# Attention's k, V and q in a pool of their own, loaded ahead; waits by tile; last additions on VectorE

## The chip, the cores and the metric

The kernel runs on one core of a Trainium2 chip. The metric is the device time of one execution in microseconds, from the median of several runs. The engines have their own instruction queues: TensorE (PE, with its weight loads as PEld), VectorE (DVE), ScalarE (ACT), GpSimd (POOL), and SyncE (SP), which here only issues transfers (DMA).

## The reference, cut to what matters

The input x is 4 x 128 x 64 x 64, in float32. Two layers follow each other.

Layer 0 normalises x by groups, runs small state-space models (a seed and a cascade of two) over the 4096 positions, and ends with a convolutional FFN per batch entry: a 128 to 256 matmul, a 3 x 3 depthwise convolution, GELU and a 256 to 128 matmul.

Layer 1 is attention and a mixture of experts over the 4096 tokens of each batch entry:

```python
t = _to_tokens(x)
t = t + _L1_attn_ref(_ln_t(t), ...)   # 4 heads of 32, softmax over 4096 keys
t = t + _L1_ffn_ref(_ln_t(t), ...)    # 8 experts of 128 to 128, top 2
```

with, inside attention,

```python
scores = jnp.einsum('bhqd,bhkd->bhqk', q, k) / jnp.sqrt(jnp.float32(HEAD_DIM))
attn = jax.nn.softmax(scores, axis=-1)
ctx = jnp.einsum('bhqk,bhkd->bhqd', attn, v)
```

## The kernel before

**Layer 0** (L1154). Positions are cut into 8 blocks of 512. The scan over seed and cascade goes block by block. The operations are recorded by a planner (`Deck`, L773): steps of several generators are interleaved by `run` (L255) in proportion to the number of steps that each is given, every recorded operation gets its place in that order as its rank, and `flush` (L911) lays the operations out with assumed costs and emits them. The emitted order is kept on PE, DVE, ACT and POOL (`manual_schedule`, L1490); SP is not in that list, so the order of its transfers is set by the framework. In the profile every recorded operation has line L1040.

The FFN of a batch entry (`ffn`, L1357) runs beside the scan of the next one. The last FFN, that of entry 3, has no scan beside it. There it is interleaved with attention's projections of entry 0 (`early`, L1526, which steps through `prepare`, L1574): for each block of 512 tokens a normalisation, then q, k and V, where q and k are split into a high part and a low part (`lower`, L1609), and all are stored in DRAM (qd, kd, vd). The FFN is entered in the interleaving with 129 steps, the projections with 47 (L1542). The pools for this part (`first`, `psf`, `last`, L1519 and L1520) are opened after those of the scan are closed (L1518). The FFN of a block ends with a sum t (L1472 on DVE, L1473 on POOL) and its store to td.

**Layer 1** (L1646). A unit is one head and one block of 512 queries: 4 entries x 8 blocks x 4 heads = 128 units. `load` (L1814) fetches a unit's keys k4 (four strips of 32 partitions, two with the high part and two with the low part, 512 KB each), its queries q4 (four strips) and its values V. For every unit there are three passes:

- maxima: 32 matmuls of 128 queries by 512 keys, each reduced on DVE (`maximum`, L1836), 44 of them ahead of the first group (LEAD);
- scores in 8 groups of 512 keys (`scores`, L1874): a matmul that subtracts the maximum (L1882), four score matmuls (L1888), the exponential on ACT (L1892), and the sums over the group's four parts on POOL (L1894, L1896), which later give the denominator;
- context: e times V (L1909), and the denominator from the sums (`total`, L1918). Both are saved to DRAM (`save`, L1901).

When the four heads of a block are done, `tail` (L1696) reads their parts back (L1699), adds the parts (L1705 to L1712), multiplies by the inverse of the denominator (L1714), applies the output projection, a second normalisation (with a product, L1733) and the experts (L1774 to L1788), and stores the block. The steps of tails and of the next entry's projections are fitted between the groups by `background` (L1946). After the loop over the groups, the first steps of the last tail are emitted and then the rest:

```python
for _, task in timed:
    next(task)
behind += [start(task) for _, task in soon]
while behind:
    advance(behind)
```

`timed` holds five steps of the last tail, which are five of its six sums, and `start` takes the sixth. `behind` holds what is left of the tail of the block before.

The constants of layer 1 (pc, 906.5 KB) are loaded twice: for the early projections on POOL's queue (L1522), and for layer 1 on ACT's (L1675).

Of the kernel before, what the change touches and what calls it, by code (L numbers as in the profile page):

```python
# [21 lines left out]
F32 = mybir.dt.float32  # L22
# [4 lines left out]
AX = mybir.AxisListType  # L27
ENG = mybir.EngineType
PSUM = bass.MemoryType.PSUM

NBATCH, C, IMG = 4, 128, 64
L = IMG * IMG
# [1117 lines left out]
def blk(k):  # L1150
    return slice(k * LB, (k + 1) * LB)


def layer0(tc, T, td, const, ident, eps, where, batches, qkv):  # L1154
# [9 lines left out]
    with ExitStack() as ctx:  # L1164
# [139 lines left out]
        class Cascade(Seed):  # L1304
# [194 lines left out]
        for s in range(-2, len(items) + 1):  # L1499
# [12 lines left out]
            if 0 < s and items[s - 1].last:  # L1512
                if pending is not None:
# [35 lines left out]
class Stores:  # L1549


    def __init__(self, pool):
        self.pool, self.q, self.k, self.v = pool, {}, {}, {}
# [92 lines left out]
def layer1(tc, T, td, const, ident, eps, where, out, batches, qkv):  # L1646
# [10 lines left out]


    nc = tc.nc
    NQT = L // 128  # L1660
    LEAD = 44
    with ExitStack() as ctx:
        fix = ctx.enter_context(tc.tile_pool(name="fix1", bufs=1))
        kvp = ctx.enter_context(tc.tile_pool(name="kv", bufs=3))
        work = ctx.enter_context(tc.tile_pool(name="work1", bufs=2))
        dram = ctx.enter_context(tc.tile_pool(name="dram1", bufs=2, space=bass.MemoryType.DRAM))
        psm = ctx.enter_context(tc.tile_pool(name="psm", bufs=3, space=PSUM))
        pss = ctx.enter_context(tc.tile_pool(name="pss1", bufs=2, space=PSUM))
        psa = ctx.enter_context(tc.tile_pool(name="psa", bufs=1, space=PSUM))
# [26 lines left out]
        def tail(b, k):  # L1696
            pa = work.tile([128, 2, 4, LB], F32, tag="parts", bufs=1, name="parts")
            for h in range(NHEAD):
                nc.sync.dma_start(out=pa[HD * h:HD * h + HD], in_=cds.pop((b, h, k)).rearrange("s i d l -> d s i l"))  # L1699
            tk = tmp("tt", bufs=2)  # L1700
            nc.sync.dma_start(out=tk, in_=td[b, :, blk(k)])
            cx = tmp("cx", bufs=1)
            for s in (1, 0):
                yield
                nc.gpsimd.tensor_add(pa[:, s, 0], pa[:, s, 0], pa[:, s, 1])  # L1705
# [4 lines left out]
                nc.gpsimd.tensor_add(pa[:, s, 2], pa[:, s, 2], pa[:, s, 3])  # L1710
                yield
                nc.gpsimd.tensor_add(pa[:, s, 0], pa[:, s, 0], pa[:, s, 2])  # L1712
            yield 0.4, False
            nc.gpsimd.tensor_mul(cx, cx, pa[:, 0, 0])  # L1714
            yield 0.0, False
            yield 0.75, True
            po = ps("ps_o")
# [12 lines left out]
            r = tmp("r")  # L1730
            rsqrt(nc, r, pv, eps)
            yield 0.4, False
            nc.gpsimd.tensor_mul(xl, xl, r)  # L1733
            yield 0.0, False
            yield 0.8, True
            pl = ps("ps_l")[:, 0:4 * NEXP]
# [77 lines left out]
        def load(u):  # L1814

            if u >= len(units):
                return
            b, h, k = units[u]
            if h == 0 and k == 0:
                while ahead or todo:  # L1820
                    if not ahead:
                        ahead.append(start(todo.pop(0)))
                    advance(ahead)
            k4 = kvp.tile([128, L], F32R, tag="k4", name="k4")
            for j in range(4):
                nc.sync.dma_start(out=k4[32 * j:32 * j + 32, :].bitcast(F32),
                                  in_=qkv.k[b][j // 2, HD * h:HD * h + HD, :])
            q4 = work.tile([128, LB], F32R, tag="q4", bufs=5, name="q4")
            for j in range(4):
                nc.sync.dma_start(out=q4[32 * j:32 * j + 32, :].bitcast(F32),  # L1830
                                  in_=qkv.q[b][j % 2, HD * h:HD * h + HD, blk(k)])
            V = kvp.tile([128, NQT, HD], F32, tag="V", name="V")
            nc.sync.dma_start(out=V.rearrange("p t d -> p (t d)"), in_=qkv.v[b][h])
            k4s[u], q4s[u], Vs[u] = k4, q4, V

        def maximum(n):  # L1836

# [36 lines left out]
        def scores(u, g, n):  # L1874

            pts = [pss.tile([128, 2, LB], F32, tag="s", name="ps_s") for _ in range(2)]
            for j in range(4):  # L1880
                rows = slice(32 * j, 32 * j + 32)
                nc.tensor.matmul(pts[j // 2][:, j % 2, :], lhsT=ones2[rows, :], rhs=mrows[u][rows, :],  # L1882
                                 start=True, stop=False)
            for j in range(4):
                if j % 2 == 0:
                    maximum(n + j // 2)
                kt = 4 * g + j
                nc.tensor.matmul(pts[j // 2][:, j % 2, :], lhsT=k4s[u][:, 128 * kt:128 * kt + 128],  # L1888
                                 rhs=q4s[u], start=False, stop=True)
# [6 lines left out]
            nc.gpsimd.tensor_add(s, s2[:, 0], s2[:, 1])  # L1896
            return e, s

        accs, dens = {}, {}
# [113 lines left out]
def emit(tc, T, where, out, batches=range(NBATCH), layers=(0, 1), td=None):  # L2013
    nc = tc.nc
    with ExitStack() as ctx:
        cp = ctx.enter_context(tc.tile_pool(name="const", bufs=1))
        ct = cp.tile([128, where["const"]["grp"][0]], F32, name="const_sb")
        nc.gpsimd.dma_start(out=ct, in_=T["const"][:, 0:where["const"]["grp"][0]])
        const = Cols(ct, where["const"])
        ident = cp.tile([128, 128], F32, name="ident")  # L2020
        make_identity(nc, ident)
        eps = cp.tile([128, 1], F32, name="eps")
        nc.gpsimd.memset(eps, 1e-5)
        qkv = Stores(ctx.enter_context(tc.tile_pool(name="qkv", bufs=2, space=bass.MemoryType.DRAM)))
# [21 lines left out]
```

## Time and profile before

| | |
|---|---|
| median of 3 runs | 8313.97 us (8304.8 to 8316.73) |
| the profiled execution | 8310.76 us, of which the span 8309.0 us |
| granted TensorE clock, mean | 0.954 |
| busy: PE, DVE, ACT, POOL | 91%, 76%, 61%, 59% of the span |
| layer 0, scan | up to about 3472 us |
| last FFN with the projections | about 3472 to 3672 us |
| attention: first maximum, first scores | 3694.0 us, 3722.4 us |
| last scores | 8248.7 us |
| POOL addition 128x1024, 128x512 (L1894, L1896) | 2385 ns, 1281 ns, 1024 of each |
| DVE maximum 128x512 (L1852) | 689 ns, 4096 of them |

The span is the profiler's, from the first to the last instruction. Times of single instructions are given in us from its start. A row of the chain or of the timeline gives start, duration, engine, tile and line, and where there is a mark "x8" the number of instructions that were merged. DMA issues appear on the queue that issues them (SPq, ACTq, POOLq) with the time of the issue, not of the transfer.

### The profile page before, as it was taken

The numbers are of one execution on the slowest core, as the hardware profiler recorded it, in microseconds if no ns is written. First come the engines' busy times: TensorE is split into PE (matmuls) and PEld (weight loads), VectorE is DVE, ScalarE is ACT, GpSimd is POOL, SyncE is SP. The second block draws the span as 40 slices with busy tenths as digits, with TensorE's granted clock in tenths as the row PEclk, the third lists the DMA queues.
The fourth block names the chain that finished last, engine by engine and source line by source line (L and its number), as shares of the span: only waits on it lengthen the run. The fifth ranks groups of instructions, "written<-read, shape, count | busy, mean of one in ns | idle before, by whom it ended". The sixth has DMA issues, their size and how long they took to land.

```text
span 8309.0 us, 191474 instructions
## 1 busy us (share of the span) xinstructions
PE 7600.4 (91%) x80284; PEld 4516.6 (54%) x80284; DVE 6299.9 (76%) x11211; ACT 5103.8 (61%) x6517; POOL 4892.5 (59%) x3441
## 2 busy tenths in 40 slices
PE   5888888888888898779999999999999999999998
PEld 3566666666666666434555555555555545555554
DVE  5676768887888788776777777777777777777775
ACT  5767767777777777545555555555555555555554
POOL 1111111211122112119999999999999999999997
PEclk7889999999999899889999999999999999999999
DMA  4221112221112121145544445444545454444442
GB/s 139 83 56 48 43 53 57 54 57 54 52 55 59 54 62 46 54 133 139 129 126 124 127 123 130 127 126 126 129 121 136 122 135 122 120 116 121 116 121 59
DMA packets 306606, 800.55 MB, mean 96 GB/s; under 512 B 43985, under 2 KB 61009, under 8 KB 288849
## 3 DMA queue, kind: packets, MB, share of 16 engines
q1 hardware_dynamic: 304848, 780.94, 35.8%
q8 instruction: 633, 10.37, 0.5%
q10 hardware_dynamic: 432, 5.12, 0.2%
q14 instruction: 229, 1.87, 0.1%
q0 software_dynamic: 464, 2.25, 0.1%
HBM read 595.19 MB, written 192.94 MB: 95 GB/s over the span
## 4 chain that ended last, share of the span: by engine, by line
PE 29%; POOL 22%; issue 3%; DVE 2%; ACT 1%; DMA 1%; SPq 0%; POOLq 0%; DVEq 0%
POOL s L1894 13%; PE ps_mx L1850 7%; PE acc L1909 6%; POOL es L1896 6%; PE ps_s L1888 6%; PE ps_s L1882 3%; PE ps_e L1798 2%; PE ps_den L1922 1%; DVE mx L1852 1%; PE ps_taps L1040 1%; PE ps_sh L1869 0%; POOL parts L1712 0%; POOL cx L1714 0%; PE ps_f L1787 0%; PE ps_f L1786 0%
## 5 line engine op out<-in xcount | busy, mean ns | idle before, releaser
L1852 DVE TENSOR_REDUCE mx<-ps_mx 128x1 f32<-128x512 f32 x4096 | 2789.8, 689 | 815.0 <-PE ps_mx L1850 807.8
L1892 ACT ACTIVATE e<-ps_s 128x1024 f32<-128x1024 f32 x2048 | 1985.3, 1022 | 1715.6 <-PE ps_s L1888 1610.8
L1894 POOL TENSOR_TENSOR s<-e 128x1024 f32<-128x1024 f32 x1024 | 2442.2, 2385 | 206.7 <-ACT e L1892 203.5
L1850 PE MATMUL ps_mx<-k,q 128*128 128x512 f32 x4096 | 1876.1, 467 | 63.5 <-DVE mx L1852 25.3
L1896 POOL TENSOR_TENSOR es<-s 128x512 f32<-128x512 f32 x1024 | 1311.7, 1281 | 80.3
L1888 PE MATMUL ps_s<-q,k 128*128 128x512 f32 x4096 | 1279.5, 394 | 0.0
L1909 PE MATMUL acc<-e,V 128*32 128x512 f32 x8192 | 1095.2, 607 | 0.0
L1850 PEld LDWEIGHTS ps_mx<-k,q 128*128 128x128 f32 x4096 | 772.7, 189 | 532.1 <-DVE mx L1852 221.9
L1040 POOL TENSOR_TENSOR zs<-y,zs 128x256 f32<-128x256 f32 (+1 forms) x288 | 302.7, 1052 | 1153.0 <-DVE y L1040 1152.2
L1888 PEld LDWEIGHTS ps_s<-q,k 128*128 128x128 f32 x4096 | 772.6, 189 | 137.8 <-issue 2.9
L1040 DVE SCALAR_TENSOR_TENSOR e<-e,gm 128x1024 f32<-128x1024 f32 (+1 forms) x576 | 668.0, 1175 | 54.8 <-ACT e L1040 53.3
L1882 PEld LDWEIGHTS ps_s<-mr,ones 32*128 32x128 f32 x4096 | 201.4, 182 | 890.5 <-ACT e L1892 411.1
L1040 ACT ACTIVATE e<-ps_d 128x1024 f32<-128x1024 f32 (+1 forms) x576 | 546.5, 975 | 86.1 <-PE ps_d L1040 63.4
L1882 PE MATMUL ps_s<-mr,ones 32*128 32x512 f32 x4096 | 531.9, 496 | 20.3 <-ACT e L1892 20.3
L1040 DVE SCALAR_TENSOR_TENSOR y<-bank,const,y 128x128 f32<-128x128 f32 (+1 forms) x1152 | 364.2, 338 | 234.4 <-PE bank L1040 233.7
L1040 PE MATMUL bank<-e,xp 64*32 64x128 f32 x17408 | 459.0, 283 | 63.6 <-DVE y L1040 51.1
L1040 PEld LDWEIGHTS bank<-e,xp 64*32 64x32 f32 x17408 | 369.4, 110 | 134.9 <-DVE y L1040 73.7
L1040 PE MATMUL ps_d<-rt,lt 32*128 32x256 f32 x4352 | 406.7, 312 | 32.3 <-ACT e L1040 10.8
L1040 PEld LDWEIGHTS ps_d<-rt,lt 32*128 32x128 f32 x4352 | 294.6, 190 | 194.0 <-issue 50.1
L1909 PEld LDWEIGHTS acc<-e,V 128*32 128x32 f32 x8192 | 161.7, 108 | 362.6 <-issue 356.5
L1805 DVE SCALAR_TENSOR_TENSOR acc<-ps_e,w,acc 128x128 f32<-128x128 f32 x896 | 312.5, 349 | 47.7 <-PE ps_e L1798 15.0
L1040 DVE SCALAR_TENSOR_TENSOR acc<-h,pb,acc 128x512 f32<-128x512 f32 x448 | 330.4, 757 | 7.5
(349 smaller groups left out, 11503.7 us busy)
## 6 DMA issues: line engine op xcount, KB each, us to landing
k<-kd SPq DMA_DIRECT2D x512, 512.0 KB
x<-hl SPq DMA_DIRECT2D x256, 256.0 KB
V<-vd SPq DMA_DIRECT2D x128, 512.0 KB
cd<-raw SPq DMA_DIRECT2D x256, 256.0 KB
parts<-cd SPq DMA_DIRECT2D x128, 512.0 KB
xin<-in_x SPq DMA_DIRECT2D x128, 256.0 KB
q<-qd SPq DMA_DIRECT2D x512, 64.0 KB
hl<-hi SPq DMA_DIRECT2D x72, 256.0 KB
```

The lines of the kernel that those rows point to most:

```text
L1040: getattr(getattr(self.nc, op.engine), name)(*[self.real(a) for a in args], **{k: self.real(a) for k, a in kw.items()})
L1798: nc.tensor.matmul(pe, lhsT=xl[:, tok], rhs=ew[:, e:e + 2, :].rearrange("p e c -> p (e c)"), start=True, stop=True)
L1805: nc.vector.scalar_tensor_tensor(acc, pe[:, 128 * j:128 * j + 128], we, acc, ALU.mult, ALU.add)
L1850: nc.tensor.matmul(p, lhsT=q4s[u][:, 128 * qt:128 * qt + 128], rhs=k4s[u][:, blk(kb)], start=True, stop=True)
L1852: nc.vector.tensor_reduce(mxs[u][:, qt, kb:kb + 1], p, AX.X, ALU.max)
L1882: nc.tensor.matmul(pts[j // 2][:, j % 2, :], lhsT=ones2[rows, :], rhs=mrows[u][rows, :], start=True, stop=False)
L1888: nc.tensor.matmul(pts[j // 2][:, j % 2, :], lhsT=k4s[u][:, 128 * kt:128 * kt + 128], rhs=q4s[u], start=False, stop=True)
L1892: nc.scalar.activation(e[:, 2 * j:2 * j + 2], pts[j], AF.Exp)
L1894: nc.gpsimd.tensor_add(s2, e[:, 0:2], e[:, 2:4])
L1896: nc.gpsimd.tensor_add(s, s2[:, 0], s2[:, 1])
L1909: nc.tensor.matmul(accs[u][32 * j:32 * j + 32, :], lhsT=Vs[u][:, 4 * g + j, :], rhs=e[:, j, :], start=g == 0, stop=g == 7)
L1922: nc.tensor.matmul(p[32 * j:32 * j + 32, :], lhsT=ones, rhs=s, start=True, stop=True)
```

## The change

One pool at the other end of SBUF ("right") now holds k4, q4, V and the constants pc. It is opened in layer 0, after the scan's pools are closed, and stays open to the end. The loading of a unit becomes a method of `Stores`, and the first unit is loaded as the last step of `early`, so within the planner's work for the last FFN. `early` has one step more (48) and is interleaved with the first 112 steps of the FFN; what the FFN has left follows. The second load of pc is gone.

The pool `work` of layer 0 is closed with the scan; the sums that the last FFN reads from it move to a pool `totals`. The pools that are opened after the scan, and those of layer 1, get `reuse_waits="tile"`: a tile waits for the former users of its own bytes, where before it waited for those of the whole pools that lay there.

The sums of the last eight groups (those of the last unit), and the six sums and two products of the last block's tail, go to VectorE instead of POOL.

```diff
         psw, dram = deck.ring(psw, 2, PSUM), deck.ring(dram, 1, bass.MemoryType.DRAM)
-        work = ring(ctx, "work", 2)
+        totals = ring(ctx, "totals", 2)
         scan = ctx.enter_context(ExitStack())
+        work = ring(scan, "work", 2)
...
-                        sums[b] = work.tile([128, NBLK], F32, tag="sums", name="sums")
+                        sums[b] = totals.tile([128, NBLK], F32, tag="sums", name="sums")
...
         scan.close()
-        pw, pp = ring(ctx, "first", 2), ring(ctx, "psf", 3, space=PSUM)
-        last = ring(ctx, "last", 2)
-        pct = pw.tile(list(T["pc"].shape), F32, tag="pc", bufs=1, name="pc")
-        nc.gpsimd.dma_start(out=pct, in_=T["pc"])
-        prepare = projections(nc, td, const, eps, Cols(pct, where["pc"]), pw,
+        qkv.heads(tc, T)
+        pw, pp = (ring(ctx, name, bufs, space=space, reuse_waits="tile")
+                  for name, bufs, space in (("first", 2, SBUF), ("psf", 3, PSUM)))
+        last = ring(ctx, "last", 2, reuse_waits="tile")
+        prepare = projections(nc, td, const, eps, Cols(qkv.pc, where["pc"]), pw,
                               ps, qkv, nc.vector)
...
                 yield
+            qkv.unit(nc, batches[0], 0, 0)
+            yield
...
-        run((pending, FFN), (deck.staged("early", early()), 5 * NBLK + 7))
+
+        run((islice(pending, 112), 112), (deck.staged("early", early()), 5 * NBLK + 8))
+        run((pending, FFN - 112))
         deck.flush(tc)
...
+    def heads(self, tc, T):
+        self.kv = self.stack.enter_context(tc.tile_pool(name="kv", bufs=3, side="right", reuse_waits="tile"))
+        self.pc = self.kv.tile(list(T["pc"].shape), F32, tag="pc", bufs=1, name="pc")
+        tc.nc.gpsimd.dma_start(out=self.pc, in_=T["pc"])
+
+    def unit(self, nc, b, h, k):
+        k4 = self.kv.tile([128, L], F32R, tag="k4", name="k4")
+        for j in range(4):
+            nc.sync.dma_start(out=k4[32 * j:32 * j + 32, :].bitcast(F32),
+                              in_=self.k[b][j // 2, HD * h:HD * h + HD, :])
+        q4 = self.kv.tile([128, LB], F32R, tag="q4", bufs=5, name="q4")
+        for j in range(4):
+            nc.sync.dma_start(out=q4[32 * j:32 * j + 32, :].bitcast(F32),
+                              in_=self.q[b][j % 2, HD * h:HD * h + HD, blk(k)])
+        V = self.kv.tile([128, L // 128, HD], F32, tag="V", name="V")
+        nc.sync.dma_start(out=V.rearrange("p t d -> p (t d)"), in_=self.v[b][h])
+        self.loaded[b, h, k] = k4, q4, V
...
-        fix = ctx.enter_context(tc.tile_pool(name="fix1", bufs=1))
-        kvp = ctx.enter_context(tc.tile_pool(name="kv", bufs=3))
-        work = ctx.enter_context(tc.tile_pool(name="work1", bufs=2))
+        fix = ctx.enter_context(tc.tile_pool(name="fix1", bufs=1, reuse_waits="tile"))
+        work = ctx.enter_context(tc.tile_pool(name="work1", bufs=2, reuse_waits="tile"))
...
-        pct = fix.tile(list(T["pc"].shape), F32, name="pc")
-        nc.scalar.dma_start(out=pct, in_=T["pc"])
-        P = Cols(pct, where["pc"])
+        P = Cols(qkv.pc, where["pc"])
...
+            adds = nc.vector if (b, k) == (batches[-1], NBLK - 1) else nc.gpsimd
...
-                nc.gpsimd.tensor_add(pa[:, s, 0], pa[:, s, 0], pa[:, s, 1])
+                adds.tensor_add(pa[:, s, 0], pa[:, s, 0], pa[:, s, 1])
...
-            nc.gpsimd.tensor_mul(cx, cx, pa[:, 0, 0])
+            adds.tensor_mul(cx, cx, pa[:, 0, 0])
...
-            k4 = kvp.tile([128, L], F32R, tag="k4", name="k4")
...
+            if (b, h, k) not in qkv.loaded:
+                qkv.unit(nc, b, h, k)
+            k4s[u], q4s[u], Vs[u] = qkv.loaded.pop((b, h, k))
...
             s2 = work.tile([128, 2, LB], F32, tag="s2", name="s2")
-            nc.gpsimd.tensor_add(s2, e[:, 0:2], e[:, 2:4])
+            adds = nc.vector if 8 * u + g >= 8 * len(units) - 8 else nc.gpsimd
+            adds.tensor_add(s2, e[:, 0:2], e[:, 2:4])
             s = tmp("es", bufs=6)
-            nc.gpsimd.tensor_add(s, s2[:, 0], s2[:, 1])
+            adds.tensor_add(s, s2[:, 0], s2[:, 1])
```

More of the change, by code (lines that the diff above doesn't have):

```diff
@@ L29 @@
 PSUM = bass.MemoryType.PSUM
+SBUF = bass.MemoryType.SB
 NBATCH, C, IMG = 4, 128, 64
@@ L1541, in layer0, with __init__ @@
         pending = deck.staged("ffn", ffn(pending, last, single("f", 4), 1, 4, taps, single("t", 2)))
-        run((pending, FFN), (deck.staged("early", early()), 5 * NBLK + 7))
+        run((islice(pending, 112), 112), (deck.staged("early", early()), 5 * NBLK + 8))
+        run((pending, FFN - 112))
         deck.flush(tc)
 class Stores:
-    def __init__(self, pool):
-        self.pool, self.q, self.k, self.v = pool, {}, {}, {}
+    def __init__(self, pool, stack):
+        self.pool, self.stack, self.q, self.k, self.v = pool, stack, {}, {}, {}
+        self.loaded = {}
     def open(self, b):
@@ L1659, in layer1 @@
     nc = tc.nc
-    NQT = L // 128
     LEAD = 44
     with ExitStack() as ctx:
-        fix = ctx.enter_context(tc.tile_pool(name="fix1", bufs=1))
-        kvp = ctx.enter_context(tc.tile_pool(name="kv", bufs=3))
-        work = ctx.enter_context(tc.tile_pool(name="work1", bufs=2))
+        fix = ctx.enter_context(tc.tile_pool(name="fix1", bufs=1, reuse_waits="tile"))
+        work = ctx.enter_context(tc.tile_pool(name="work1", bufs=2, reuse_waits="tile"))
         dram = ctx.enter_context(tc.tile_pool(name="dram1", bufs=2, space=bass.MemoryType.DRAM))
-        psm = ctx.enter_context(tc.tile_pool(name="psm", bufs=3, space=PSUM))
-        pss = ctx.enter_context(tc.tile_pool(name="pss1", bufs=2, space=PSUM))
-        psa = ctx.enter_context(tc.tile_pool(name="psa", bufs=1, space=PSUM))
+        psm = ctx.enter_context(tc.tile_pool(name="psm", bufs=3, reuse_waits="tile", space=PSUM))
+        pss = ctx.enter_context(tc.tile_pool(name="pss1", bufs=2, reuse_waits="tile", space=PSUM))
+        psa = ctx.enter_context(tc.tile_pool(name="psa", bufs=1, reuse_waits="tile", space=PSUM))
         def ps(name):
             return psm.tile([128, LB], F32, tag="m", name=name)
-        pct = fix.tile(list(T["pc"].shape), F32, name="pc")
-        nc.scalar.dma_start(out=pct, in_=T["pc"])
-        P = Cols(pct, where["pc"])
+        P = Cols(qkv.pc, where["pc"])
         ones = fix.tile([128, 32], F32, name="ones")
@@ L1709, in tail @@
                 yield
-                nc.gpsimd.tensor_add(pa[:, s, 2], pa[:, s, 2], pa[:, s, 3])
+                adds.tensor_add(pa[:, s, 2], pa[:, s, 2], pa[:, s, 3])
                 yield
-                nc.gpsimd.tensor_add(pa[:, s, 0], pa[:, s, 0], pa[:, s, 2])
+                adds.tensor_add(pa[:, s, 0], pa[:, s, 0], pa[:, s, 2])
             yield 0.4, False
-            nc.gpsimd.tensor_mul(cx, cx, pa[:, 0, 0])
+            adds.tensor_mul(cx, cx, pa[:, 0, 0])
             yield 0.0, False
@@ L1732, in tail @@
             yield 0.4, False
-            nc.gpsimd.tensor_mul(xl, xl, r)
+            adds.tensor_mul(xl, xl, r)
             yield 0.0, False
@@ L1823, in load @@
                     advance(ahead)
-            k4 = kvp.tile([128, L], F32R, tag="k4", name="k4")
[L1825 to L1834, printed above, removed]
+            if (b, h, k) not in qkv.loaded:
+                qkv.unit(nc, b, h, k)
+            k4s[u], q4s[u], Vs[u] = qkv.loaded.pop((b, h, k))
         def maximum(n):
@@ L2023, in emit @@
         nc.gpsimd.memset(eps, 1e-5)
-        qkv = Stores(ctx.enter_context(tc.tile_pool(name="qkv", bufs=2, space=bass.MemoryType.DRAM)))
+        qkv = Stores(ctx.enter_context(tc.tile_pool(name="qkv", bufs=2, space=bass.MemoryType.DRAM)), ctx)
         if td is None:
```

## The prediction

> **What bounds the kernel now.** I read the page first (busy shares and slices), then busy time by stretch, then the chain of waits around the two seams of the program (start and end of the last FFN) and over the last 100 us, and last the timeline of single instructions there. Three stretches of the busy table (columns: stretch, length, busy us and count of PE, PE loads, DVE, ACT, POOL, granted clock, DMA share, GB/s):
>
> ```profile
> core 0: us, PE busy (x) PEld busy (x) DVE busy (x) ACT busy (x) POOL busy (x), PEclk, DMA share, GB/s
> ...
> 3500.00:3550.00 50.00, 47.65 (x133) 21.28 (x133) 43.48 (x65) 34.90 (x59) 1.64 (x1) 1.00 0.38 122
> 3680.00:3694.00 14.00, 0.00 (x0) 0.02 (x1) 0.00 (x0) 0.00 (x0) 0.00 (x0) 0.50 1.02 210
> 4000.00:4300.00 300.00, 296.63 (x1702) 156.06 (x1694) 234.91 (x429) 163.54 (x195) 284.41 (x177) 1.00 0.51 130
> ```
>
> Attention (last row) is set by TensorE: 99% busy at full clock, and the chain in it is matmuls only. The change touches none of these matmuls nor their order, so some 4500 us of the span stay as they are. It acts at the seams. In the middle row no engine computes for 14 us while the DMA engines are full (share 1.02). The chain over both seams:
>
> ```profile
> 3482.06 6.98 DMA xin<-in_x
> ...
> 3489.07 0.81 ACT xin L1040
> ...
> 3490.45 2.08 PE ps_var L1040 x2
> ...
> 3674.24 3.94 DMA kd<-kh
> 3678.24 7.05 DMA k<-kd
> 3685.31 8.71 DMA k<-kd
> 3694.02 0.77 PE ps_mx L1850
> ```
>
> The last FFN begins with a wait for x (until 3489.07), and attention with a wait for k: the last VectorE operation of layer 0 ends at 3671.58, block 7's k is stored and lands at 3678.18, then unit 0 is loaded, and the first maximum starts at 3694.0. And the end of the chain:
>
> ```profile
> 8233.72 0.26 POOL w L1769
> 8234.03 0.97 PE ps_w L1774 x4
> ...
> 8254.80 1.27 POOL es L1896
> ...
> 8257.25 0.70 DVE raw L1928
> ...
> 8260.03 4.62 DMA parts<-cd
> 8264.88 1.27 POOL parts L1705
> ...
> 8272.57 1.27 POOL cx L1714
> ```
>
> From 8209.7 to 8234 the chain is POOL alone: it runs behind with its sums (s at 8237.59 for an e that ended at 8233.73) and holds TensorE at 8234.03. Then it is late again (es ends at 8256.07, the last e at 8250.62), and after the DMA round trip six sums and a product lie on the path.
>
> **1. First unit loaded early.** The moved step issues nine DMAs on SP: four of k (2.10 MB), four of q (0.26), one of V (0.52); rows of before: 1.71 + 2.31 + 0.32 us of issue. When can they go? k's source is complete when block 7's low part has landed. The FFN has 113 steps (1 + 8 x 14), and before they were mixed 129 to 47 with the projections; block 7's k is projection step 45, so due at FFN step 123, after the FFN's end. Now it is 112 to 48: step 45 is due at FFN step 105. The FFN's sums t at steps 99, 107 and 113 lie at 3644.1, 3655.8 and 3668.2, so step 105 was at about 3653. By then seven more projection steps are done (45, not 38), 1.4 blocks of ten VectorE operations of 0.69 us: 9.7 us later, 3662. Projections ran ahead of their due step by 13 to 17 us in blocks 0 to 5 and by 4 in block 6; I take 3, so kf of block 7 at 3659 (before: 3669.45). From kf to the issue of the last store block 6 took 3.9 us (3657.41 to 3661.31), landing 3.9 (row DMA kd<-kh): 3667. From the first k issue to the first maximum before: 3694.01 - 3678.24 = 15.8 us, with V's 0.52 MB ahead in the queue, 2.5 us at 210 GB/s. In the new code V is last: 13.3 us. Maxima begin at 3680.3: **-13.7 us**. Bounds: if block 7 is only 4 us earlier and V still first, -4; if all lands before layer 0 ends at 3671.6, -22.4, and more isn't there, since DVE and PE still have the FFN before the maxima. The FFN's end is latency (conv, gelu, two matmuls, t), and may slip to some 3676 without cost.
>
> Here the rate decides, and the Trainium skill has two. "SBUF — State Buffer", section on the DMA setup-cost knee, gives 2 us plus bytes at 436 GB/s: k and q in 7.4 us, a gain of 20. Its section on the port swizzle says that a transfer into 32 partitions, as each strip of k is, reaches half of the ports. The row has 210 GB/s at a full DMA share, so I take the row.
>
> What the issues pass: on SP they wait for the landing of kd, and behind them stand the store of the last td block and unit 1's loads. Nothing in attention reads this td block early, and unit 1 is needed only 32 maxima (about 21 us) after unit 0. The pc load (906 KB) falls away at 3669 on ACT's queue; the other stays on POOL's queue behind t (L1473) at 3478, 28 us before its first reader: nothing.
>
> **2. Tiles wait for their own bytes.** Before, outs and tk of the last FFN were issued at 3472.5, right behind the scan's last store, and xin and gf only behind the store of t (3478.27), the third xin at 3482.06. With the work pool now closed with the scan and waits by tile, most of these loads have old owners that end before 3462, while SP stands idle from 3450.1 to 3472.0. If they go then, ln_r waits for DVE outs alone (3482.87 + 0.75 = 3483.6) and starts at 3483.7 instead of 3489.8: ps_var at 3484.5, not 3490.45: **-5.9 us**, which the following FFN (PE 95%, DVE 87% busy) passes on. If one of the three xin falls on bytes of the old FFN's acc, t or xin (28 KB of the pool, used until 3478), nothing is gained: bounds 0 and -6. I take the gain, with somewhat better than even chances. Nothing is added to attention's own buffers, which turn over as before.
>
> **3. Additions on VectorE.** In the last eight groups DVE has only the expert sums (0.74 us per group of 3.26). A 128x512 addition has 0.68 us there (row L1724: 0.69) against POOL's 1.28, 128x1024 by two of its pitches 1.2 against 2.39: 1.9 us per group, it fits. POOL is freed, so w (L1769) comes at about 8226.6 and ps_w no longer waits: 1.9 us, and the cold matmuls after it (1.94 for eight instead of 1.07), less what the group needs anyhow, 2.3 in all. The last e ends at 8248.3, es at 8250.2, raw starts at 8251.4 instead of 8257.25: -5.9. parts land at 8259.0.
>
> Now the queue. After the loop the code issues the last tail's six sums first and then what is left of the tail before it: in before that is VectorE work from 8258.03 to 8268.29 (twenty expert sums, four o), **10.3 us that lay under the round trip**. On VectorE's in-order queue the six sums now wait for parts in front of it. So: 8259.0 + six sums (4.0) + 10.3 + the product 0.7 = 8274.0, against 8273.83 before. The product xl (L1733) then gains 0.6, and TensorE, just busy, may start ps_o warm (1.0 of 2.09): **-0.9 us**. Bounds: +4 (POOL's lag was no limit) and -4 (the rest runs faster with its matmuls done beforehand).
>
> The skill speaks against this part: by "SBUF — State Buffer", section "Who interferes with whom", a VectorE operation with two SBUF inputs and a GpSimd operation that reads SBUF shut each other out. The trace agrees: gate (L1759) took 1.10 us at 8221.19 beside POOL's es and 0.17 alone at 8288.97. POOL's two last sums end at 8226.0, the first of DVE's could start at 8223.8: 2.2 us late by the rule, nothing without it; 1.3 us per group are free, so it is made up within two groups. I add nothing.
>
> **The sum.** -13.7 - 5.9 - 0.9 = -20.5 on the profiled execution of 8310.76 us (span 8309.0 and 1.8 around it) is 8290.3. The median of the runs is 8313.97, 3.2 above that execution: 8313.97 - 20.5 = 8293.5 us.
>
> **Rivals.** (a) Half of it: block 7 comes out only 4 to 6 us earlier, because the denser projections push each other as block 6 did (4 us ahead only, spacing 31 us), and x comes no sooner: -8, 8306 us. For it: SP stores of block 7 stood 5 us in the queue before. Chance 0.28. (b) The change doesn't do what it says: SP's order, which is not written out by hand, leaves the nine issues behind the last store of layer 0, so that the 13 us of transfer stay bare, and the end brings nothing: 8313 us. Against it: the issues stand ahead of that store in the new code. Chance 0.12. (c) Slower: the last FFN stretches. PE is 95% busy in it, and 48 projection steps in 112 make it denser by 18%; if each of the eight blocks then waits for one projection chain (v to q to k, 5 to 6 us in the timeline), 8 x 5.5 = 44, less 20: +24, 8338 us. It decides from 20.5 / 8 = 2.6 us per block on. Against it: total work is the same, and DVE has 13% free. Chance 0.05. The forecast itself: 0.55.
>
> **The numbers.** Runs of before spread over 12 us (0.14%), so I count 0.2% (16.6 us, 8297.3) as what can be told from no change. The forecast's own range is 8283 to 8301, and about 0.03 of its chance lies above 8297.3; rival (a) puts 0.04 below. Faster 0.56, same 0.39, slower 0.05. The 80% range leaves out a tenth at each end: 8281 (k landed before layer 0 ends, full gain on x and at the end: -32) to 8312.
>
> **What would show it.** Right: first maximum between 3670 and 3680 (both gains), no stretch over 10 us without compute after layer 0; first k issue before the FFN's last t; xin normalised before 3480. At the end: raw about 6 us closer to the last ps_s, then VectorE idle for 7 us before parts and the expert sums after them. Wrong: k issues after 3672; xin still behind td<-t; a mean spacing of the FFN's t over 24 us; the product cx more than 28 us after the last e's end.

## The result, and the profile after

The changed kernel took 8280.9 us (median of six runs, 8270.66 to 8287.86), the kernel before 8303.84 us beside it (six runs, 8289.81 to 8316.73). The ratio is **0.9969, 95% interval 0.9956 to 0.9982** (of the means; the medians lie 22.9 us apart): 25.7 us less (15 to 37). Faster was forecast, and is what came. The forecast time, 8293.5 us, is 12.6 too high, and the measured one lies just under the forecast's range of 8281 to 8312; 10.1 of the 12.6 is the kernel before, which had 8313.97 in the three runs shown and 8303.84 in the six of the comparison. The forecast difference of 20.5 us lies inside the interval. But the terms of the sum do not hold: one gave much more than forecast, one cost time instead of saving it, one came out near nothing, and one saving was not in the sum at all.

Stretches cut at the same events show it. Each kernel was profiled twice, unedited (the second executions are the last runs of two series below):

| stretch, us | before | before again | after | after again | mean change |
|---|---|---|---|---|---|
| up to scan's last ys store | 3472.00 | 3460.86 | 3468.41 | 3472.90 | same code |
| to the last FFN's first ps_var | 18.45 | 17.33 | 19.87 | 20.03 | +2.1 |
| FFN and projections, to layer 0's last VectorE operation | 181.13 | 181.54 | 174.82 | 177.11 | -5.4 |
| to the first maximum | 22.43 | 22.29 | 0.45 | 0.15 | -22.1 |
| to the first e of the last eight groups (see below) | 4524.60 | 4519.76 | 4517.49 | 4520.75 | same code |
| to the end of the last e | 32.01 | 30.50 | 29.07 | 29.07 | -2.2 |
| to the end | 58.38 | 59.82 | 62.49 | 62.59 | +3.4 |

The fifth row ends at an exponential that every profile shows with a wait of 1.81 or 1.82 us for POOL's es, just ahead of the last unit. The rows with changed code add up to -24.2 us. The two rows of unchanged code move by 7 and 12 us among these four executions, so the first two spans alone (8309.0 and 8272.6) overstate the change by 11 us.

Other profiles below repeat parts of this code. The kernel before's last two rows stand in one more profile ("the dealing alone"), the changed kernel's in three (the first three experiments). Added up, the two rows take 90.3 to 90.8 us in the three profiles of before, and 91.6, 91.7, 89.4, 89.0 and 89.4 us in the five of the changed kernel. So the end moved by +1.2 us in the two columns above, and by some -1.1 in the three others: near nothing, and not the 1.2 us lost that the table alone shows.

Busy time by stretch, changed kernel (columns as before):

```profile
core 0: us, PE busy (x) PEld busy (x) DVE busy (x) ACT busy (x) POOL busy (x), PEclk, DMA share, GB/s
3500.00:3550.00 50.00, 47.39 (x138) 21.84 (x139) 42.99 (x65) 35.22 (x61) 1.64 (x1) 1.00 0.52 169
3650.00:3664.00 14.00, 8.27 (x17) 3.07 (x16) 9.52 (x13) 3.55 (x5) 2.46 (x2) 0.88 0.95 223
4000.00:4300.00 300.00, 296.70 (x1703) 155.39 (x1702) 234.44 (x428) 165.24 (x198) 285.86 (x178) 1.00 0.51 130
```

The first and last rows are close to those of before (the DMA share of the first is 0.52 instead of 0.38). The middle one is new: the DMA engines are as full as in the 14 idle us of before (share 0.95 beside 1.02), but TensorE and VectorE work in it. The chain at the start of the FFN and at the start of attention, changed kernel:

```profile
3473.03 1.27 POOL t L1041
...
3474.32 0.32 SPq L1041
...
3475.16 7.10 DMA tk<-td
...
3482.28 4.60 DMA xin<-in_x
...
3486.90 0.81 ACT xin L1041
...
3488.28 2.07 PE ps_var L1041 x2
...
3660.43 1.90 PE ps_f L1041 x2
3662.33 1.22 issue
3663.55 0.78 PE ps_mx L1868
```

From the FFN's last matmul the chain goes straight to the first maximum; no k is in it. At the FFN's start the wait for x is still there, and now leads through tk back to POOL's t. The end of the chain:

```profile
8210.14 1.24 DVE s L1913
...
8214.14 0.69 DVE raw L1947
...
8216.94 4.43 DMA parts<-cd
...
8221.56 0.69 DVE parts L1731
...
8225.76 2.07 PE ps_e L1824 x4
...
8233.42 0.72 PE ps_f L1813 x2
...
8237.72 0.69 DVE cx L1740
```

POOL is gone from it, as meant. But between the sums (to 8225.5) and the product cx lie 12 us of the previous tail's expert work.

### The profile page after: what moved, and what is told of

It is laid out like the page before. It is cut to its first block, busy times and chain, and to the rows that moved or that the text cites. A ratio compares the mean times of both kernels' runs of the same rounds, so it can differ in the third digit from the quotient of the medians.

```text
span 8272.6 us, 191432 instructions
## 1 busy us (share of the span) xinstructions
PE 7587.7 (92%) x80284; PEld 4508.1 (54%) x80284; DVE 6304.5 (76%) x11235; ACT 5099.1 (62%) x6513; POOL 4848.1 (59%) x3417
## 4 chain that ended last, share of the span: by engine, by line
PE 32%; POOL 20%; issue 3%; DVE 2%; ACT 1%; DMA 0%; POOLq 0%; SPq 0%; DVEq 0%; ACTq 0%
POOL s L1913 12%; PE ps_mx L1868 8%; PE acc L1928 7%; PE ps_s L1906 6%; POOL es L1915 6%; PE ps_s L1900 3%; PE ps_e L1824 2%; PE ps_den L1941 2%; DVE mx L1870 1%; PE ps_taps L1041 1%; PE ps_sh L1887 0%; PE ps_f L1813 0%; PE ps_f L1812 0%; POOL cx L1740 0%; POOL parts L1738 0%
## 5 line engine op out<-in xcount | busy, mean ns | idle before, releaser
L1900 PE MATMUL ps_s<-mr,ones 32*128 32x512 f32 x4096 | 532.7, 496 | 20.5 <-ACT e L1910 20.5
L1041 PE MATMUL ps_d<-rt,lt 32*128 32x256 f32 x4352 | 404.3, 311 | 32.3 <-ACT e L1041 11.4
```

The source lines that it names most:

```text
L1041: getattr(getattr(self.nc, op.engine), name)(*[self.real(a) for a in args], **{k: self.real(a) for k, a in kw.items()})
```

## The experiments

"Gap" is the time from layer 0's last VectorE operation to the first maximum; "FFN start" that from scan's last ys store to the first ps_var. "Dealing" is how the steps of the projections are spread over the steps of the last FFN. Ratios are to the kernel before.

### Without the call

```diff
-            qkv.unit(nc, batches[0], 0, 0)
             yield
```

> The changed kernel without the call that loads attention's first unit inside the last FFN; the pool at the far end and the waits by tile stay, so attention's own code issues the same loads. Theory A (a pool whose bytes are free is enough: the compiler's ordering of SP's queue then puts the loads forward by itself, all but what sits behind the last store of layer 0): from layer 0's last VectorE operation to the first maximum 5 to 8 us, where the changed kernel has 0.45 and the kernel before 22.4; the time about 6 us above the changed kernel. Theory B (the call is what brings the loads forward): 14 us or more between the two, and some 14 us above the changed kernel.

Ratio 0.9979 (0.9970 to 0.9987). The gap is 10.32 us: without the call 12 of the 22 us are saved already, and the call brings the other 10. SP's queue puts the first strip of k forward to 3654.85 and the second to 3663.95 without being told to, but the other two and V stay behind layer 0's last store, and this is the chain there:

```profile
3668.77 1.31 POOL t L1041
...
3670.09 0.32 SPq L1041
...
3670.46 0.43 SPq L1579
...
3670.93 7.88 DMA k<-kd
...
3678.95 0.78 PE ps_mx L1867
```

t is added, its store is issued at 3670.09, and only then two strips of k and V. Theory A named the place rightly and undersized it (5 to 8 us expected): after the store still lie the issue of a strip and its 7.9 us of transfer.

### The old dealing of the projections, in the changed kernel

```diff
-        run((islice(pending, 112), 112), (deck.staged("early", early()), 5 * NBLK + 8))
-        run((pending, FFN - 112))
+        run((pending, FFN), (deck.staged("early", early()), 5 * NBLK + 8))
```

> The changed kernel with the projections dealt over all 129 steps of the last FFN again, not over the first 112. Theory A (the earlier projections are what hid the loads entirely and what shortened the FFN): block 7's k is ready at about 3660 to 3666 us instead of 3646, FFN and projections take 6 us longer (181 instead of 174.8), and the first maximum comes 8 to 14 us after layer 0's last VectorE operation; 14 to 20 us above the changed kernel. Rival B (the pool and the call do it alone): FFN and projections 175, the gap below 3 us, the time the same.

Ratio 0.9975 (0.9966 to 0.9984). Theory A was right on the gap alone, and rival B on nothing. The FFN did not get longer but shorter, 168.65 us, and the gap grew to 8.15 us: 176.8 together, against 175.3 and 177.3 in the changed kernel. Block 7's kf comes at 3651.93, its stores and a td store stand ahead of k in SP's queue, and the last strip decides:

```profile
3656.60 0.38 SPq L1041
...
3657.07 0.47 SPq L1041
...
3658.51 11.78 DMA k<-kd
...
3670.43 0.78 PE ps_mx L1867
```

So the dealing is needed to hide k fully, but what it does to the FFN is another matter, to which the clock below is the key.

### Waits for whole pools, in the changed kernel

```diff
-        self.kv = self.stack.enter_context(tc.tile_pool(name="kv", bufs=3, side="right", reuse_waits="tile"))
+        self.kv = self.stack.enter_context(tc.tile_pool(name="kv", bufs=3, side="right"))
```

and the same for every other pool of the change.

> The changed kernel with every new pool waiting for all of the pool it replaces, as before. Theory A (the tile waits gain nothing at the start of the FFN, since its loads stand behind scan's last t store in SP's queue anyway): from the last ys store to the first ps_var 19 to 21 us (19.87 changed, 18.45 before), the gap before the first maximum under 3 us, the time the same within 0.1%. Rival B (they do gain): the first ps_var 3 us or more later, or the first maximum 3 us or more after layer 0's end, and the time up by as much.

Ratio 0.9970 (0.9960 to 0.9981), the changed kernel's own. The gap is 0.18 us. So it is not the tile waits that freed k, V and q. That it is the pool's place, where no buffer of the last FFN lay, is what remains; no run moved the pool alone. FFN start is 21.02 us; counted from the td store of t, where the paths part, 14.93 us against 13.96 and 13.86 (13.3 to 13.7 in five other profiles of that code). That some 1 us, from one profile, is all that the tile waits give.

### The dealing alone, in the kernel before

```diff
-        run((pending, FFN), (deck.staged("early", early()), 5 * NBLK + 7))
+        run((islice(pending, 112), 112), (deck.staged("early", early()), 5 * NBLK + 7))
+        run((pending, FFN - 112))
```

> The kernel before with only the dealing of the projections over the first 112 steps. Theory A (this alone shortens the FFN, and attention's start still waits for its pool): FFN and projections 174 to 176 us instead of 181.1, the gap before the first maximum still 16 to 22 us, the time 5 to 10 us below the kernel before. Rival B (the FFN got shorter because attention's loads or the narrower waits changed its queues): FFN and projections 180 to 182, the time unchanged.

Ratio 0.9983 (0.9975 to 0.9990), 14 us less. Theory A holds in kind, and undersized both savings (174 to 176 us of FFN and 5 to 10 us of time expected): FFN and projections take 169.94 us, and the gap is still 17.16 us, because with the pool of before the loads of q and V wait for the landing of layer 0's last store (in the chain of that run: td<-t for 7.26 us, then q's issues, then V for 7.42 us). This small edit brings half of the whole change's gain, and the pool then has less left to bring. The parts overlap and can't be added.

### The last tail's sums on GpSimd again

```diff
-                adds.tensor_add(pa[:, s, 0], pa[:, s, 0], pa[:, s, 1])
+                nc.gpsimd.tensor_add(pa[:, s, 0], pa[:, s, 0], pa[:, s, 1])
```

and so for all six; the last unit's sums and the products stay on VectorE.

> The changed kernel with the last tail's six sums of partials on GpSimd again; the last unit's sums and the two products stay on VectorE. Theory A (the sums on VectorE hold up the rest of the previous tail behind them in VectorE's queue, TensorE runs dry meanwhile, and the product waits for both): the rest starts before the partials have landed, and the product cx starts 7 to 8 us after the first sum instead of 16.2; the end 8 to 10 us earlier, the time about 0.1% below the changed kernel. Rival B (the rest of the previous tail is slow for another reason, such as its own TensorE work): cx still 14 us or more after the first sum, the time the same.

Ratio 0.9963 (0.9951 to 0.9975). cx starts 7.63 us after the first sum, and the last e's end to the program's end takes 54.85 us instead of 62.5 (60 in the first three experiments). Theory A holds: the rest of the previous tail starts at 8226.9, while the parts are in flight (first sum at 8234.0). In the time this doesn't stand out, since the interval is 0.12% (10 us) wide to each side.

### The rest of the previous tail ahead of the sums

```diff
+        while behind:
+            advance(behind)
         for _, task in timed:
             next(task)
         behind += [start(task) for _, task in soon]
```

> The changed kernel with the rest of the previous tail written out ahead of the last tail's sums; all additions stay on VectorE. Theory A (only the order on VectorE's queue was wrong): the rest runs while the partials are in flight, then 4.0 us of sums: cx 4.7 to 7 us after the first sum, and the first sum at most 3 us later after the raw copy than in the changed kernel (7.4); 7 to 10 us off the end. Rival B (the rest needs the time anyway): raw copy to cx stays at 22 to 24 us.

Ratio 0.9959 (0.9943 to 0.9974). VectorE in that run (timeline: start, duration, engine, line, operation):

```profile
8217.23 0.29 DVE L1814 TENSOR_TENSOR o<-ps_f,tt 128x128 f32<-128x128 f32 x1
...
8226.16 0.29 DVE L1814 TENSOR_TENSOR o<-ps_f,tt 128x128 f32<-128x128 f32 x1 [0.58 <-PE ps_f L1813]
8226.37 0.68 DVE L1731 TENSOR_TENSOR parts<-parts 128x512 f32<-128x512 f32 x1
...
8230.41 0.69 DVE L1740 TENSOR_TENSOR cx<-cx,parts 128x512 f32<-128x512 f32 x1
```

The rest takes 9.2 us (8217.23 to 8226.45) and lies under the parts' round trip; behind the sums it took 12.3 us. TensorE is still at full clock from the last unit (0.98 granted from 8217 to 8227): two ps_f matmuls (ident, acc) take 0.49 us here and 0.80 in the changed kernel. The first sum comes 2.4 us later after the raw copy, cx 4.04 us after it, and last e to end is 52.78 us, 9.7 less than in the changed kernel and 7.1 to 7.6 less than in the first three experiments. Only the order on VectorE's queue was wrong; GpSimd isn't needed for it.

### All additions on GpSimd

```diff
-            adds = nc.vector if 8 * u + g >= 8 * len(units) - 8 else nc.gpsimd
+            adds = nc.gpsimd
...
-            adds = nc.vector if (b, k) == (batches[-1], NBLK - 1) else nc.gpsimd
+            adds = nc.gpsimd
```

> The changed kernel with all additions and products on GpSimd as before (the rest of the change stays). Theory A (step 3 gains in the last unit and loses more in the tail): last unit 32 us instead of 29.1, last e to raw 6.6 instead of 4.0, first sum to cx 7.7 instead of 16.2, cx to the end 36.4 instead of 34.9; in sum 1 to 2 us less from the last eight groups to the end, so no difference in the time that can be measured. Rival B (VectorE pays): 3 us or more longer than the changed kernel over the same stretch.

Ratio 0.9959 (0.9944 to 0.9974). Last unit 32.04 us, last e to end 58.50: 90.54 in all. The kernel before has 90.39 and 90.32, the changed kernel 91.56 and 91.66, which is theory A's loss of 1.1 us: 3.0 saved in the last unit, 4.0 lost from there to the end. But the first three experiments have the same code there as the changed kernel and 89.0 to 89.4. So the third part of the change lies between a loss of 1.1 and a gain of 1.5 us, and what differs is the clock behind the sums (see the next run).

### The changed kernel again

> The changed kernel once more, unedited, for what differs between executions. Theory A (the 174.8 us of FFN and projections are their order of work plus one stretch at a lower granted clock, 0.74 from 3620 to 3640 us, that falls elsewhere or nowhere in another execution): between 168 and 182 us in this one, moving with the clock. Rival B (the order alone sets it): 174 to 176 us again. In both, the gap before the first maximum under 1 us, and first sum to cx 16 us.

Ratio 0.9964 (0.9950 to 0.9977). FFN and projections took 177.11 us, with the same dip of the clock behind the same pause: the order sets it, not chance, though 2.3 us move. Gap 0.15, first sum to cx 16.16 us. In the first three experiments, whose code there is the same, the latter is 14.4 to 14.9 us, and from there to the end it is 1 us less too. There the clock comes back within the rest: without the call ps_f takes 0.79 us at 8248.42 and 0.48 at 8253.24, and in the changed kernel 0.79 from 8227.76 to the last.

### Scan's last t store on GpSimd's queue (with the rest ahead of the sums)

```diff
-                nc.sync.dma_start(out=td[b, :, blk(k)], in_=t)
+                store = nc.sync if depth or k < NBLK - 1 else nc.gpsimd
+                store.dma_start(out=td[b, :, blk(k)], in_=t)
```

> The kernel with the rest of the previous tail ahead of the last sums, and besides scan's last t store on GpSimd's queue instead of SP's, so that the last FFN's first loads no longer stand behind it. Theory A (the place in SP's queue is what made the tile waits worthless): outs, tk and xin go out within 2 us of the last ys store, and the first ps_var comes 12 to 14 us after it (18 to 20 with the store on SP, 18.45 before). Theory B (the bytes of the first tk tile are those that GpSimd's last addition reads, and the tile wait holds SP there as long as the store did): outs goes at once, tk and all behind it 5 us or more after the ys store, and the first ps_var 16 to 19 us after it.

Ratio 0.9960 (0.9945 to 0.9974). SP's queue in that run:

```profile
3458.97 0.32 SPq L1041 DMA_DIRECT2D td<-ys  x1
3461.03 0.32 SPq L1041 DMA_DIRECT2D outs<-td  x1
3463.00 0.32 SPq L1041 DMA_DIRECT2D tk<-td  x1
3463.37 0.42 SPq L1041 DMA_DIRECT2D xin<-in_x  x1
```

The store is out of the way, and tk still goes only at 3463.00, when POOL's addition (3461.71, 1.26 us) ends at 3462.97. FFN start is 17.14 us, against 17.87 in the one profile of the same kernel with the store on SP. Theory B: the bytes hold nearly as long as the store did (tk goes 4.0 us after the ys store, 5 or more expected).

### Besides, the projections' pool at the far end

```diff
-        pw, pp = (ring(ctx, name, bufs, space=space, reuse_waits="tile")
-                  for name, bufs, space in (("first", 2, SBUF), ("psf", 3, PSUM)))
+        pw = ring(ctx, "first", 2, side="right", reuse_waits="tile")
+        pp = ring(ctx, "psf", 3, space=PSUM, reuse_waits="tile")
```

> As the kernel before it, with the pool of the projections' tiles at the far end too, so that the first tk and xin wait for TensorE and ScalarE only, and not for GpSimd's last addition. Theory A (bytes and queue together were the bound): outs at once, tk and the first two xin about 4 us after the last ys store instead of 6, the third xin after tk has landed, some 9 to 10 us; the first ps_var 14 to 16 us after the ys store, 3 to 5 us less than with SP's order. Rival B (GpSimd's addition or the transfers themselves are the bound): 17 us or more. With the tail's order from the earlier run, last e to the end 53 us, and the time 0.40 to 0.50% below the kernel before.

Ratio **0.9941 (0.9929 to 0.9954)**, 8256.57 us: 48 us below the kernel before, and faster than the changed kernel. SP's queue:

```profile
3468.45 0.32 SPq L1041 DMA_DIRECT2D td<-ys  x1
3468.82 0.42 SPq L1041 DMA_DIRECT2D outs<-td  x1
3469.34 0.41 SPq L1041 DMA_DIRECT2D tk<-td  x1
3469.84 0.38 SPq L1041 DMA_DIRECT2D xin<-in_x  x1
...
3475.10 0.43 SPq L1041 DMA_DIRECT2D xin<-in_x  x1
```

The first three loads go out within 1.4 us of the ys store (in the changed kernel 7.3), and the third xin at 3475.10, 6.7 us after it (13.9). FFN start is 12.53 us, 7.4 less than in the changed kernel and better than theory A (14 to 16) had it. Of the prediction's 5.9 us, 5.4 were there to be had: from another place for the tiles, and with the store on another queue. The place alone, with the store on SP, was not run. By the rows of the first table this version changes the start by -5.4 us, FFN and projections by -9.9, the gap by -22.0, the last unit by -2.2 and the end by -5.7.

### The kernel before again

> The kernel before once more, unedited, for what differs between executions. Theory A (the 181.1 us of FFN and projections contain one stretch at a lower granted clock, which falls by chance): 170 to 185 us, moving with the clock. Rival B (the order alone sets it): 180 to 182 us. In both: the first maximum 20 to 24 us after layer 0's last VectorE operation, first sum to cx 7.7 us, last e to the end 58.4 us.

Ratio 1.0000 (0.9991 to 1.0009). FFN and projections 181.54 us, gap 22.29, first sum to cx 7.70 us: as before. Last e to end is 59.82, a miss of 1.4, with 30.50 in the last unit instead of 32.01; the two together are 90.3 both times.

### The clock in the FFN

The thirteen profiles have FFN and projections between 168.7 and 181.5 us with the same operations. I cut each into 18 equal slices and added up, per slice, its length times what the granted clock lacked of 1:

| kernel | time | lost by the clock | the rest |
|---|---|---|---|
| before, twice | 181.1, 181.5 | 16.7, 16.9 | 164.4, 164.6 |
| changed, twice | 174.8, 177.1 | 10.7, 13.4 | 164.1, 163.7 |
| old dealing | 168.7 | 5.7 | 162.9 |
| dealing alone | 169.9 | 9.8 | 160.1 |
| waits for pools | 174.5 | 12.1 | 162.4 |
| the version at 8256.57 us | 171.4 | 7.2 | 164.2 |

The rest is within 4.5 us everywhere; of the 5.4 us between before and after, the clock accounts for 4.7. This is bookkeeping: a slow clock costs its full share only where TensorE sets the pace. It is no merit of the new dealing as such: the old dealing in the changed kernel and the new one in the kernel before are both shorter still, at 168.7 and 169.9. Where the clock goes, in the kernel before, then in the changed kernel, and in the one with the old dealing last (columns as before):

```profile
3580.00:3600.00 20.00, 19.21 (x50) 9.03 (x50) 13.51 (x20) 12.26 (x20) 1.64 (x1) 0.87 0.28 89
3600.00:3620.00 20.00, 18.58 (x37) 8.03 (x38) 12.72 (x20) 12.12 (x20) 0.00 (x0) 0.74 0.38 126
```

```profile
3616.00:3626.00 10.00, 6.94 (x19) 2.96 (x18) 9.86 (x14) 5.11 (x9) 1.64 (x1) 0.86 0.48 170
3626.00:3636.00 10.00, 10.00 (x20) 4.25 (x18) 3.49 (x6) 5.74 (x10) 0.00 (x0) 0.63 0.21 68
3636.00:3646.00 10.00, 10.00 (x31) 4.97 (x30) 8.82 (x11) 2.27 (x6) 1.92 (x2) 1.00 0.13 52
```

```profile
3616.00:3626.00 10.00, 8.06 (x26) 3.37 (x24) 9.89 (x15) 5.60 (x10) 1.64 (x1) 1.00 0.52 184
3626.00:3636.00 10.00, 10.00 (x29) 4.70 (x28) 6.83 (x11) 7.35 (x13) 0.15 (x1) 1.00 0.16 54
```

In the changed kernel TensorE waits at 3620.1 for 3.06 us for ACT's ln_r; the granted clock then is 0.50 for some 10 us, in which TensorE is 100% busy and does 20 matmuls, where 29 fit in the other. All nine profiles with this 3.06 us pause inside the FFN have the dip behind it. With the old dealing the pause there is 1.75 us, and no dip follows. In each profile of the kernel before there are three pauses of 2.2 us, and the clock drops behind two of them.

## Why the prediction was right or wrong

**What failed.** Besides the 10.1 us by which the sum started too high, three terms failed: step 1's time for block 7's kf was mis-sized (8.4 us too little gained), the FFN's own length was put at nothing (it gave 5.4), and step 2's saving of 5.9 was a loss of 2.1. Of the signs of being wrong listed in advance, one showed for the last of these: xin still went behind td<-t.

**Step 1, right in kind, undersized: -13.7 forecast, -22.1 measured**, the upper bound of the step (-22.4). The term that failed is block 7's kf. I had it at 3659, 10 us earlier than before; it came at 3646.04, 177.6 us after the ys store instead of 197.4. Two parts of that term were off. FFN step 105 lies at about 3652.5 (between the sums at 3643.0 and 3655.7), where it lay before; the 9.7 us that I added for seven more projection steps ahead of it did not come. And the projections led their due step by 6.5 us, not by the 3 that I took. k's two high strips went out at 3649.52, on the landing of their source, the low ones at 3653.10 and V at 3658.22, behind the stores of V, and q at 3508.82 with the projections of block 0. I had put q into the transfer that counts; it needs no more than block 0. From kf to the first maximum it is 17.5 us (21.3 in the forecast), and layer 0 ended at 3663.10, so it fits: with kf 6.7 us later against layer 0's end (old dealing) a gap of 8.15 us is left.

```profile
3508.82 1.71 SPq L1041 DMA_DIRECT2D q<-qd  x4
...
3649.52 0.78 SPq L1041 DMA_DIRECT2D k<-kd  x2
3651.20 1.85 SPq L1041 DMA_DIRECT2D vd<-vf  x4
3653.10 0.94 SPq L1041 DMA_DIRECT2D k<-kd  x2
3658.22 0.34 SPq L1041 DMA_DIRECT2D V<-vd  x1
```

The rate taken from the row, 210 GB/s, was a better choice than the 436 GB/s of the Trainium skill ("SBUF — State Buffer", section on the DMA setup-cost knee): over 3650 to 3664 the engines moved 223 at a share of 0.95. That the gain of 20 estimated from 436 comes nearer to 22.1 is luck, since the loads simply went out earlier.

**A saving that the sum did not have: -5.4 in the FFN.** I wrote that its end "may slip to some 3676". It came at 3663.1. The order of the work moved TensorE's pauses, and the stretches at half clock moved with them. The profile of before showed it (the two rows above: 0.87 and 0.74 granted between 3580 and 3620), and I read busy shares there and not the clock.

**Step 2, wrong: -5.9 forecast, +2.1 measured.** The sentence that failed is "most of these loads have old owners that end before 3462". SP keeps its queue in order, and in the changed kernel every load of the FFN stands behind the store of t, outs and tk too, which before went 5.8 us ahead of it:

```profile
3472.48 0.32 SPq L1040 DMA_DIRECT2D outs<-td  x1
3472.85 0.46 SPq L1040 DMA_DIRECT2D tk<-td  x1
3478.27 0.32 SPq L1040 DMA_DIRECT2D td<-t  x1
```

The third xin then waits for tk's landing (3475.16 and 7.10), so the path from the store to ps_var grew from 12.2 to 14.0 us (11.4 to 12.2 in three profiles of that code before, 13.3 to 14.0 in seven of the code after). The forecast's own way out, a load that falls on bytes of the old FFN, came true as well, for tk. The "bounds 0 and -6" excluded a loss, and nothing spoke for excluding one: a queue whose order is made by the framework can come out worse. The last two versions show that both the store and tk's bytes, which POOL's last addition still used, held the loads; with both moved, -5.4 against the kernel before's mean of 17.9.

**Step 3, right in structure: -0.9 forecast, +1.2 measured in the two executions of the changed kernel, -0.9 to -1.4 in three others with the same end.** The last unit gained 2.2 to 2.9 (forecast 2.3). From the last e's end to cx I had 25.0 us, and it was 27.6 (25.9 to 26.5 in the three): e to raw 4.0 instead of 3.1, and the rest of the previous tail 12.3 (10.4 to 10.9) instead of 10.3. In the profile of before, where the 10.3 came from, the granted clock was 0.75 to 1.00 over the rest (8256 to 8268); behind the sums TensorE has been idle for 10.1 us from 8215.65, and its clock is 0.50 in the whole of 8220 to 8250. I had named the queueing itself, and not its order as something to repair: with it repaired the same part is worth -8.

**The skill's rule on VectorE and GpSimd** ("SBUF — State Buffer", section "Who interferes with whom", that a VectorE operation with two SBUF inputs and a GpSimd operation that reads SBUF shut each other out) was forecast to cost nothing. It shows at the hand-over between the two engines: VectorE's first s and es take 1.80 and 1.66 us beside POOL's last s and es, 1.22 and 0.69 two groups on.

```profile
8186.34 1.80 DVE L1913 TENSOR_TENSOR s<-e 128x1024 f32<-128x1024 f32 x1 [6.10 <-ACT e L1910]
8188.17 1.66 DVE L1915 TENSOR_TENSOR es<-s 128x512 f32<-128x512 f32 x1
...
8190.32 1.22 DVE L1913 TENSOR_TENSOR s<-e 128x1024 f32<-128x1024 f32 x1
```

VectorE has caught up by 8193.5, where it waits for ACT's e again, as forecast.

**The rivals.** (b), loads left behind layer 0's last store, is what happens without the call, for two strips and V: 10 us. (c) did not come: FFN and projections took 174.8 and 177.1 us, against 181.1 and 181.5. (a) was right that x comes no sooner, and wrong that block 7 comes late. That the sum came within 4 us of the stages' -24.2 is luck: 8.4 and 5.4 us that it lacked on one side, 8.0 and 2.1 on the other.

## What to carry to other kernels

A load is early only if three things allow it: the bytes of its tile, its place in an in-order queue, and its source; freeing one of them (waits by tile) does little while another stands (here a store behind a late addition, then that addition's own bytes). When work moves to another engine, look at what is already queued there, and put what has no wait ahead of what has one; that order alone was worth 7 to 10 us here. And where TensorE pauses for 2 to 3 us in a dense stretch, count the 7 to 10 us at half clock that can stand behind it, not the pause alone.

## What was not expected of the hardware

In the dense part of the FFN a pause of TensorE of 3.06 us was followed in nine of nine profiles by 10.2 us (in two of them 6.8) at a granted clock of 0.50 (in the changed kernel from 3623 to 3633 us), though TensorE was busy throughout; after pauses of 2.2 us it happened in four of seven cases, and not after two of 1.75. The cost, half of that time, is 3 to 5 us, as much as the pause or more.

Where the pause falls tells the four cases from the three. In all thirteen traces the moments at which the granted clock changes lie on a grid of 3.41 us, within 0.02 us. The four pauses of 2.2 us with a dip behind them lie wholly inside one step of that grid. The three without one are cut by it, with at most 1.92 us inside one step; the nine long pauses have at least 2.05 us inside one step, and the two of 1.75 at most 1.43. So a little shift in the order of work can bring or spare a dip. This is not the whole rule: two pauses of 1.2 us were followed by 3.4 us at 0.50, and near the FFN's start, where TensorE is less busy, so were five of nine pauses of 1.5 us, by 3.4 or 6.8 us. That the pause is the trigger is read from these coincidences; no run put a pause there or took one alone away.
